# One layer of recurrent attention and routed experts on one core: how gathered rows are turned, how block 0 is projected, and how the recurrence is clipped

## The chip, the cores and the metric

The kernel runs on one core of a Trainium2 chip. The metric is the device time of one execution in microseconds (us). Before the change three runs gave a median of 363.4 us (362.94 to 363.56).

## What is computed

2048 tokens of 512 channels are normalized, and two branches are added to them:

```
xn = layernorm(x)                                  # (2048, 512), float32
r, v, k = split(xn @ W_rvk.T)                      # W_rvk (1536, 512)
for each token t:                                  # per channel; w = -exp(decay), u = first
    no = max(o, u + k);  A = exp(o - no);  B = exp(u + k - no)
    y  = (A * p + B * v) / (A * q + B)
    o2 = max(w + o, k);  A2 = exp(w + o - o2);  B2 = exp(k - o2)
    p, q, o = A2 * p + B2 * v,  A2 * q + B2,  o2
attention = (sigmoid(r) * y) @ W_out.T
probs = softmax(xn @ classifier.T)                 # 12 choices: 8 experts, 4 that hand xn through
top 2 of probs + bias, weights 1.5 * probs
ffn = sum of weight * down_e(silu(gate_e(xn)) * up_e(xn)) over a token's experts, + xn * weight of the 4
out = x + attention + ffn
```

## The kernel before

**Layout.** Tokens come in four blocks of 512 (TB). Each block is normalized row by row and turned on TensorE to xnT (channels on the partitions). The recurrence runs along the tokens, with 128 channels on the partitions, so there are 16 units (block b, channel group c); unit (b, c) needs (b-1, c). The rows of xn are also stored to DRAM (xs).

**Products k, v, r.** Direct products (half_k and project, L267 and L313) take four k-steps of 128x512 per output. For the rest, two outputs (k and v, or r of two channel groups) are made by seven products in place of eight (seven L476, sevens L560): sums of token halves (sum_tokens, S1 to S4) and of weights (T, R) are multiplied, each product is two k-steps of 256 columns, ScalarE copies the results from PSUM, and VectorE adds two of them later (the adds owed, L501, L624 and L637). In block 0, units 0 and 1 (LEAD = 2) are made directly, units 2 and 3 by seven, and r of all four directly.

**One unit's recurrence, scan(b, c), L336.** VectorE scans o2 = max(w + o, k) (L351), makes a2 = w + o - o2 (L353) and b2 = k - o2 (L354); ScalarE takes Exp of both (L356, L357); VectorE makes the two running sums (L363, L365), multiplies (L364), keeps the state (L372, L373), combines (L374 to L376), and later takes reciprocals (L380) and multiplies (L382). These steps are stages of a generator, given out one by one.

**Experts.** After routing, the places of the tokens are sorted by expert into 23 tiles of 128 rows; two are mixed from several experts. For tile i: gather (GpSimd's indirect DMA, token_i from L961) brings the rows xg; they are turned to xgT; up (L1096) multiplies them with the gate and up weights gw that SP has fetched (pg, 16 products of 128x128); activate takes Tanh and two VectorE operations; finish multiplies with dw (po) and scatters the rows, added to out. Tile 0 is turned on TensorE (turn, L1070: px, then a ScalarE copy). For all others flip (L1079) lets ScalarE split the float32 rows into their 16-bit halves (L1082), a DMA on SP's queue transposes the 16-bit array (L1084), and unite (L1087) lets ScalarE put the halves together (L1090).

**Order.** The whole is scheduled by hand: every engine runs its instructions in the order in which the program gives them out. Ahead of the experts, products are put between the routing steps with fill(n), owed adds with emit(n). Then a table (L1301 to L1338) of due times is filled by plan(): stages of the recurrence every UNIT, groups of four product steps, attention groups at places named in `after`, and the two halves of every tile every `spread`; it is sorted and given out. First_half(i) multiplies and activates tile i; second_half(i) unites tile i+1, flips i+2 and finishes i-1. k and v have five buffers each (kvp); the PSUM banks of p2, p3, pr and gu are single once block 0 is done. SP's queue holds, in order: the loads of x and the weights, the stores of xs, the weights gw and dw of tiles 0 and 1 (the second gw waits for which_late, L1272), then per tile flip, dw and gw. The last block's attention (L1244, L1232) ends the program.

Of the kernel before, what the change touches and what calls it, by code (L numbers as in the profile page):

```python
# [29 lines left out]
U16 = mybir.dt.uint16  # L30
# [5 lines left out]
P = 128  # L36
T = 2048
C = 512
# [21 lines left out]
QW = 32  # L60


@with_exitstack
def layer(ctx: ExitStack, tc: tile.TileContext, x, w_rvk, w_out, decay, first, cls, ebias, gu, down, out):
# [17 lines left out]
    dram = pool("dram", 1, space=bass.MemoryType.DRAM)  # L82
    psum = dict(space=bass.MemoryType.PSUM)
# [7 lines left out]
    def change_banks():  # L91
        early.close()
        for name, n in (("gu", 1), ("p2", 1), ("p1", 2), ("p3", 1), ("pr", 1)):
            banks[name] = pool(f"ps_{name}", n, **psum)
# [30 lines left out]
    load_w(2)  # L125
# [3 lines left out]
    load_x(2)  # L129
    load_w(1)  # L130
    load_x(3)
    load_w(0)
# [132 lines left out]
    first_k = {}  # L265

    def half_k(c, h):  # L267
        if h == 0:
            first_k[c] = ps_mm.tile([P, TB], F32, tag="mm", name=f"pk0_{c}")
        hs = slice(h * HALF, (h + 1) * HALF)  # L270
        for k in range(CC):
            nc.tensor.matmul(
                first_k[c][:, hs],
                wrvk_sb[2][:, k, c * P : (c + 1) * P],
                xnT[0][:, k, hs],
                start=(k == 0),
                stop=(k == CC - 1),
                skip_group_check=True,
            )
        if h == 1:  # L280
            kvr[0, c, "k"] = kvp.tile([P, TB], F32, tag="k", name=f"k0_{c}")
            nc.scalar.copy(kvr[0, c, "k"], first_k[c])
# [30 lines left out]
    def project(b, c, parts=(("k", 2), ("v", 1), ("r", 0))):  # L313

        n = f"{b}_{c}"
        for name, m in parts:
            ps = ps_mm.tile([P, TB], F32, tag="mm", name=f"p{name}{n}")
            for k in range(CC):
                nc.tensor.matmul(  # L319
                    ps,  # L320
                    wrvk_sb[m][:, k, c * P : (c + 1) * P],
                    xnT[b][:, k, :],
                    start=(k == 0),
                    stop=(k == CC - 1),
                )
                if k < CC - 1:
                    yield
            t = (erp if name == "r" else kvp).tile([P, TB], F32, tag=name, name=f"{name}{n}")
            if name == "r":
                nc.scalar.activation(t, ps, AF.Exp, scale=-1.0)  # L330
            else:
                nc.scalar.copy(t, ps)
            kvr[b, c, name] = t
            yield

    def scan(b, c):  # L336
# [9 lines left out]
        obv = wk1.tile([P, 3, TB + 1], F32, tag="obv", name=f"obv{n}")  # L346
        nc.vector.tensor_copy(obv[:, :, 0:1], s[:, 0:3].unsqueeze(2))
        o, bs, bvs = (obv[:, m, 0:TB] for m in range(3))
        o2, b2, bv = (obv[:, m, 1 : TB + 1] for m in range(3))
# [3 lines left out]
        nc.vector.scalar_tensor_tensor(a2, o, w, o2, ALU.add, ALU.subtract)  # L353
        nc.vector.tensor_sub(b2, k, o2)  # L354
        yield
        nc.scalar.activation(a2, a2, AF.Exp)  # L356
        nc.scalar.activation(b2, b2, AF.Exp)  # L357
# [3 lines left out]
        sums = wk1.tile([P, 2, TB], F32, tag="sums", name=f"sums{n}")  # L361
        sq, sp = sums[:, 0, :], sums[:, 1, :]
        nc.vector.tensor_tensor_scan(sq, bs, a2, s[:, 3:4], ALU.add, ALU.mult)  # L363
        nc.vector.tensor_mul(bv, b2, v)  # L364
# [3 lines left out]
        if b > 0:  # L368
            nc.scalar.activation(er, er, AF.Exp, scale=-1.0)
        num = yT[b][:, c, :]  # L370
        if b + 1 < NTB:
            nc.vector.tensor_copy(s[:, 0:3].unsqueeze(2), obv[:, :, TB : TB + 1])  # L372
            nc.vector.tensor_copy(s[:, 3:5].unsqueeze(2), sums[:, :, TB - 1 : TB])  # L373
        nc.vector.scalar_tensor_tensor(sq, b2, cf, sq, ALU.mult, ALU.add)  # L374
        nc.vector.scalar_tensor_tensor(er, er, 1.0, sq, ALU.add, ALU.mult)
        nc.vector.scalar_tensor_tensor(num, bv, cf, sp, ALU.mult, ALU.add)  # L376
        yield
        def divide(h):
# [45 lines left out]
    def sum_r_weights(first):  # L424
        if first:
            for n in (2, 3, 4):
                rsum[n] = sump.tile([P, 2, 2, P], F32, tag=f"R{n}", name=f"R{n}")
# [3 lines left out]
        else:  # L431
            nc.vector.tensor_add(rsum[2], rsum[3], r_weights(0, 0))
# [43 lines left out]
    def seven(b, c):  # L476

        n = f"{b}_{c}"
        cs = slice(c * P, (c + 1) * P)

        def bank(pool_, tag, name):
            return pool_.tile([P, TB], F32, tag=tag, name=f"{name}{n}")

        def place(pool_, name):
            kvr[b, c, name] = pool_.tile([P, TB], F32, tag=name, name=f"{name}{n}")
            return kvr[b, c, name]

        def multiply(ps, m, begin, end):
            a, w = factors(b, m)
            for k in range(2):  # L490
                nc.tensor.matmul(  # L491
                    ps[:, :HALF],
                    w[:, k, cs],
                    a[:, k, :],
                    start=(begin and k == 0),
                    stop=(end and k == 1),
                    skip_group_check=True,
                )

        def add(dst, src):  # L500
            nc.vector.tensor_add(dst, dst, src)  # L501

        def r_step(k):
            nc.tensor.matmul(  # L504
                pr, wrvk_sb[0][:, k, cs], xnT[b][:, k, :], start=(k == 0), stop=(k == CC - 1)
            )

        def next_sums(ns):
            if c == CC - 1 and b + 1 < NTB:
                for m in ns:  # L510
                    owe(lambda m=m: sum_tokens(b + 1, m))

        p1 = bank(ps_mm, "mm", "p1_")
        multiply(p1, 1, True, False)
        k = place(kvp, "k")
        nc.scalar.copy(k[:, :HALF], p1[:, :HALF])
        yield
        emit_owed()
        pr = bank(ps_tr, "tr", "pr")
        r_step(0)  # L520
        yield
        r_step(1)
        yield
        multiply(p1, 6, False, False)
        v = place(kvp, "v")
        nc.scalar.copy(v[:, :HALF], p1[:, :HALF])
        yield
        p3 = bank(ps_mm, "mm", "p3_")
        multiply(p3, 5, True, False)
        more = five.tile([P, TB], F32, tag="more", name=f"more{n}")  # L530
        nc.scalar.copy(more[:, HALF:], p3[:, :HALF])
        yield
        p2 = bank(ps_gu, "gu", "p2_")
        multiply(p2, 2, True, True)
        owe(lambda: add(k[:, :HALF], p2[:, :HALF]))
        next_sums((1, 2))
        yield
        multiply(p1, 7, False, False)
        nc.scalar.copy(v[:, HALF:], p1[:, :HALF])
        next_sums((3,))  # L540
        yield
        r_step(2)
        emit_owed()
        yield
        r_step(3)
        r = place(erp, "r")
        nc.scalar.activation(r, pr, AF.Exp, scale=-1.0)
        yield
        multiply(p1, 4, False, True)
# [3 lines left out]
        nc.scalar.copy(more[:, :HALF], p3[:, :HALF])  # L553
        owe(lambda: add(v, more))
        next_sums((4,))
        yield

# [851 lines left out]
```

## Time and profile before

| | |
|---|---|
| median of three runs | 363.4 us |
| the profiled execution | 362.48 us, its span 360.7 us, TensorE clock 1.00 |
| TensorE, VectorE, ScalarE, GpSimd busy | 354.0, 306.8, 159.0, 90.3 us |
| products pg of the tiles (L1109) | 79.1 us, products by seven (L592, nine groups) 129.8 us, attention (L1244) 54.1 us |
| ScalarE's copies for the turned rows | L1082 23.0 us (x22), L1090 25.6 us (x22) |
| VectorE's L354 / L351 / L363 / L365 | 11.0 / 20.4 / 20.5 / 20.6 us (x16 each) |
| DMA | 84.46 MB, 234 GB/s; packets of SP's queue 56.2% of 16 engines' span, of GpSimd's 25.1% |

The profile counts a float32 matmul as two instructions. A group's line reads: line, engine, operation, out<-in, shapes, count | busy us, mean ns of one | idle time before them and what ended it. The chain of work that ended last is followed back from the last instruction, in pieces of start, length and what. In a timeline a line is start, length, engine, line, operation. DVE is VectorE, ACT ScalarE, POOL GpSimd, PE TensorE, PEld its weight loads, SP the engine that issues most DMAs.

### The profile page before, as it was taken

Reading aid. Unit: us, or ns where it says so; the run is one execution under the profiler, and the core shown is the slowest. Engines: PE = TensorE matmul, PEld = TensorE weight load, DVE = VectorE, ACT = ScalarE, POOL = GpSimd, SP = SyncE. Lnnn points to the kernel's source line nnn. Section 1 sums busy time; section 2 is a strip of 40 time slices with the busy share of each in tenths; the row PEclk is TensorE's granted clock in tenths of the full one; section 3 lists DMA queues with packets and bytes.
Section 4 is the critical chain, followed back from the end, with each engine's and each line's share of the span. In section 5 each row is a group of like instructions: output and inputs, shape, how many; then the busy total and the mean of one; then the engine's idle time right before and its main releaser. Section 6 shows DMA issues by size and latency. Waiting matters only on the chain.

```text
span 360.7 us, 5328 instructions
## 1 busy us (share of the span) xinstructions
PE 354.0 (98%) x1850; PEld 256.7 (71%) x1850; DVE 306.8 (85%) x531; ACT 159.0 (44%) x308; POOL 90.3 (25%) x118
## 2 busy tenths in 40 slices
PE   8999999999999999999999999999999999999996
PEld 3764578799865877547877688988776988854344
DVE  5879889959999997899695799997989589979971
ACT  3576222354643645525545454546453546432000
POOL 6000300431312232321321433323322124221130
PEclk9999999999999999999999999999999999999999
DMA  8999950795869699967999968979979986924782
GB/s 282 398 356 363 331 174 2 245 323 135 254 196 248 147 367 301 276 215 189 281 281 334 294 189 216 309 147 306 284 226 262 236 173 167 337 55 58 177 139 95
DMA packets 47132, 84.46 MB, mean 234 GB/s; under 512 B 26496, under 2 KB 26880, under 8 KB 43328
## 3 DMA queue, kind: packets, MB, share of 16 engines
q1 hardware_dynamic: 39792, 64.05, 56.2%
q0 software_dynamic: 7312, 20.06, 25.1%
q8 instruction: 15, 0.25, 0.3%
q14 instruction: 13, 0.11, 0.1%
HBM read 63.25 MB, written 19.27 MB: 229 GB/s over the span
## 4 chain that ended last, share of the span: by engine, by line
PE 73%; DVE 17%; DMA 5%; ACT 2%; issue 1%; SPq 0%; DVEq 0%; ACTq 0%
PE pg L1109 19%; PE p L592 17%; PE po L1057 8%; PE pr L592 7%; PE pw L1244 7%; DVE r L380 4%; PE p L491 3%; DMA x<-in_x_dram 3%; DMA wrvk<-in_w_rvk_dram 2%; PE pr L504 2%; PE pr L319 2%; DVE sums L365 2%; DVE sums L363 2%; PE p2r L592 1%; PE po L1061 1%
## 5 line engine op out<-in xcount | busy, mean ns | idle before, releaser
L1109 PEld LDWEIGHTS pg<-xgT,gw 128*128 128x128 f32 x672 | 78.1, 192 | 3.7 <-ACT xgT L1090 1.6
L1109 PE MATMUL pg<-xgT,gw 128*128 128x128 f32 x672 | 79.1, 275 | 0.2 <-ACT xgT L1090 0.2
L1145 POOL DMA_INDIRECT out_dram<-yo,to_i x23 | 40.4, 1758 | 142.9 <-ACT yo L1141 28.7
L1244 PE MATMUL pw<-wout_sb,yT 128*128 128x512 f32 x120 | 54.1, 593 | 0.7 <-DVE xrows L1256 0.6
L380 DVE RECIPROCAL r<-r 128x256 f32<-128x256 f32 x32 | 53.7, 1719 | 0.0
L1244 PEld LDWEIGHTS pw<-wout_sb,yT 128*128 128x128 f32 x120 | 22.3, 190 | 25.5 <-issue 24.8
L1057 PE MATMUL po<-dw,act 128*128 128x512 f32 x84 | 39.5, 592 | 0.0
L1015 POOL DMA_INDIRECT xg<-xs,token_i x23 | 26.4, 1148 | 44.6 <-DVE empty L963 25.2
L1121 ACT ACTIVATE act<-pg 128x256 f32<-128x256 f32 x23 | 8.8, 384 | 65.0 <-PE pg L1109 60.4
L1122 DVE SCALAR_TENSOR_TENSOR act<-act,pg 128x256 f32<-128x256 f32 x23 | 9.6, 417 | 21.0 <-ACT act L1121 21.0
L1090 ACT COPY xgT<-xq 128x1024 uint16<-128x1024 uint16 x22 | 25.6, 1161 | 2.6 <-DMA xq<-xp 2.6
L1057 PEld LDWEIGHTS po<-dw,act 128*128 128x128 f32 x84 | 16.0, 190 | 13.7 <-issue 12.7
L592 PE MATMUL p<-xnT,wrvk 128*128 128x256 f32 x96 | 24.7, 380 | 0.7 <-DVE k L624 0.7
L592 PE MATMUL p<-S,wrvk 128*128 128x256 f32 x96 | 24.7, 380 | 0.0
L592 PE MATMUL p<-S,T 128*128 128x256 f32 x96 | 24.6, 379 | 0.0
L363 DVE TENSOR_TENSOR_SCAN sums<-obv,state,a 128x512 f32<-128x512 f32 x16 | 20.5, 1280 | 4.1 <-ACT obv L357 4.0
L1082 ACT COPY xp<-xg 128x1024 uint16<-128x1024 uint16 x22 | 23.0, 1047 | 0.0
L592 PEld LDWEIGHTS p<-xnT,wrvk 128*128 128x128 f32 x96 | 18.0, 190 | 6.0 <-issue 2.6
L592 PEld LDWEIGHTS p<-S,T 128*128 128x128 f32 x96 | 18.2, 190 | 5.0 <-issue 2.9
L365 DVE TENSOR_TENSOR_SCAN sums<-obv,state,a 128x512 f32<-128x512 f32 x16 | 20.6, 1288 | 0.6
L592 PEld LDWEIGHTS p<-S,wrvk 128*128 128x128 f32 x96 | 17.9, 190 | 4.3 <-issue 1.4
L351 DVE TENSOR_TENSOR_SCAN obv<-wdec,state,k 128x512 f32<-128x512 f32 x16 | 20.4, 1277 | 0.0
(262 smaller groups left out, 576.1 us busy)
## 6 DMA issues: line engine op xcount, KB each, us to landing
gw<-in_gu_dram SPq DMA_DIRECT2D x25, 1024.0 KB, 7.4
dw<-in_down_dram SPq DMA_DIRECT2D x25, 512.0 KB, 4.9
x<-in_x_dram SPq DMA_DIRECT2D x16, 256.0 KB, 6.4
xs<-x SPq DMA_DIRECT2D x16, 256.0 KB, 4.6
wrvk<-in_w_rvk_dram SPq DMA_DIRECT2D x3, 1024.0 KB, 7.2
xrow<-xs SPq DMA_DIRECT2D x8, 256.0 KB, 7.3
out_dram<-xrow POOLq DMA_DIRECT2D x8, 256.0 KB, 8.2
xrows<-xs SPq DMA_DIRECT2D x8, 256.0 KB, 6.4
```

The lines of the kernel that those rows point to most:

```text
L351: nc.vector.tensor_tensor_scan(o2, w.to_broadcast([P, TB]), k, s[:, 0:1], ALU.add, ALU.max)
L363: nc.vector.tensor_tensor_scan(sq, bs, a2, s[:, 3:4], ALU.add, ALU.mult)
L365: nc.vector.tensor_tensor_scan(sp, bvs, a2, s[:, 4:5], ALU.add, ALU.mult)
L380: nc.vector.reciprocal(er[:, hs], er[:, hs])
L592: nc.tensor.matmul(dst, rows_(k), a[:, k, :], start=(first and k == 0), stop=(k == 1), skip_group_check=True,)
L1015: nc.gpsimd.indirect_dma_start(out=xg, out_offset=None, in_=xs, in_offset=bass.IndirectOffsetOnAxis(ap=token[:, column(i) : column(i) + 1] ...
L1057: nc.tensor.matmul(out_, lhs[:, c, :], rhs[0][:, c, :], start=(c == 0), stop=(c == last))
L1082: nc.scalar.copy(xp, st[i]["xg"].bitcast(U16).rearrange("p (c h) -> p h c", h=2))
L1090: nc.scalar.copy(xgT.bitcast(U16).rearrange("p c (t h) -> p c t h", h=2), st[i]["xq"].rearrange("p (h c) t -> p c t h", h=2),)
L1109: nc.tensor.matmul(pg[:, c // IC, c % IC * P : (c % IC + 1) * P], w[0][:, k, rs], xgT[:, k, :], start=(k == 0), stop=(k == CC - 1),)
L1145: nc.gpsimd.indirect_dma_start(out=out, out_offset=bass.IndirectOffsetOnAxis(ap=index, axis=0), in_=yo[ps], in_offset=None, compute_op=ALU ...
L1244: nc.tensor.matmul(po, yT[b][:, c, j * P : (j + 1) * P], wout_sb[:, c, :], start=(c == 0), stop=(c == CC - 1),)
```

## The change

Three things change, with the due times around them.

1. **Rows turned by way of DRAM and VectorE.** turn on TensorE, flip and unite go. For every tile, spread_rows writes xg to DRAM as four column quarters (512-byte pieces), load_rows reads them back so that each group of 32 partitions holds one quarter of all 128 rows (2 KB per partition), and turn transposes 32x32 blocks on VectorE. The channels of the gate and up weights are permuted on the host to match. xgT has two buffers for one. turn(i+1) stands at the end of first_half(i), the load of tile i+2 and the write of i+3 in second_half(i).
2. **Block 0.** r of units 0 and 1 is multiplied first, in halves (half_r), then r of units 2 and 3 (project_r), and k and v of all four by seven products, interleaved (first_four). Weights are loaded in the order r, k, v, and block 3 of x ahead of k and v. More adds are owed ahead of the tiles: emit(2) before the weights of the choices, emit(4) for emit(2) after which_i.
3. **Clipping.** VectorE makes a2 = w + o - k, one operation; ScalarE makes b2 = Exp(-Relu(a2)) and then a2 = Exp(-Relu(-a2)), in two stages. L354 goes; the state is five columns of one tile and copied at once; the multiply with v stands before the first running sum. r of block 0 is copied, and Exp taken in scan.

The due times: UNIT 16.5 for 16.75, tiles from 8 on for 4, stages at (0, 4.5, 6, 7.5, 12, 14). The core of the diff:

```diff
@@ scan
-        obv = wk1.tile([P, 3, TB + 1], F32, tag="obv", name=f"obv{n}")
-        nc.vector.tensor_copy(obv[:, :, 0:1], s[:, 0:3].unsqueeze(2))
+        obv = wk1.tile([P, 5, TB + 1], F32, tag="obv", name=f"obv{n}")
+        nc.vector.tensor_copy(obv[:, :, 0:1], s.unsqueeze(2))
...
-        nc.vector.scalar_tensor_tensor(a2, o, w, o2, ALU.add, ALU.subtract)
-        nc.vector.tensor_sub(b2, k, o2)
+        nc.vector.scalar_tensor_tensor(a2, o, w, k, ALU.add, ALU.subtract)
         yield
-        nc.scalar.activation(a2, a2, AF.Exp)
-        nc.scalar.activation(b2, b2, AF.Exp)
+        nc.scalar.activation(b2, a2, AF.Relu)
+        nc.scalar.activation(b2, b2, AF.Exp, scale=-1.0)
         yield
+        nc.scalar.activation(a2, a2, AF.Relu, scale=-1.0)
+        nc.scalar.activation(a2, a2, AF.Exp, scale=-1.0)
+        yield
...
+        nc.vector.tensor_mul(bv, b2, v)
         nc.vector.tensor_tensor_scan(sq, bs, a2, s[:, 3:4], ALU.add, ALU.mult)
-        nc.vector.tensor_mul(bv, b2, v)
         nc.vector.tensor_tensor_scan(sp, bvs, a2, s[:, 4:5], ALU.add, ALU.mult)
...
-        nc.vector.scalar_tensor_tensor(sq, b2, cf, sq, ALU.mult, ALU.add)
-        nc.vector.scalar_tensor_tensor(er, er, 1.0, sq, ALU.add, ALU.mult)
+        nc.vector.scalar_tensor_tensor(a2, b2, cf, sq, ALU.mult, ALU.add)
+        nc.vector.scalar_tensor_tensor(er, er, 1.0, a2, ALU.add, ALU.mult)
@@ block 0
+    def first_four():
+        steps = {name: sevens(0, c, False)[0] for c, name in enumerate("ABCD")}
+        order = "A1 B1 A2 A6 B6 B2 A7 B7 A4 B4 C2 C1 D1 A5 D2 B5 C6 D6 A3 C7 B3 D7 C5 D5 C4 D4 C3 D3"
+        for name in order.split():
+            steps[name[0]][int(name[1])]()
+            yield
...
     def all_products():
-        for name, m in (("v", 1), ("r", 0)):
-            for u in range(LEAD):
-                yield from project(*units[u], ((name, m),))
-        for u in range(LEAD, CC):
-            yield from seven(*units[u])
+        for c in (2, 3):
+            yield from project_r(0, c)
+        yield from first_four()
@@ pair
+        if (b, c) == (1, 0):
+            order = "A1 R1 A2 A5 A6 R2 A3 A7 R5 R6 A4 B1 R7 R3 B6 B5 R4 B7 B3 B2 B4".split()
@@ routing
     nc.vector.tensor_scalar(far, real, -FAR, FAR, ALU.mult, ALU.add)
+    emit(2)
...
     which_i = place_tiles()
-    emit(2)
+    emit(4)
@@ tiles
+    def spread_rows(i):
+        q = dram_q.tile([P // SQ, P, P], F32, tag="quarters", name=f"quarters{i}")
+        nc.sync.dma_start(q.rearrange("g p c -> p g c"), st[i]["xg"].rearrange("p (g c) -> p g c", c=P))
+        st[i]["quarters"] = q
+
+    def load_rows(i):
+        xq = ex_p.tile([P, C], F32, tag="xq", name=f"xq{i}")
+        nc.sync.dma_start(xq, st[i]["quarters"].rearrange("g (i h) c -> (g i) (h c)", h=P // SQ))
+        st[i]["xq"] = xq
+
     def turn(i):
...
+        xgT = ex_p.tile([P, CC, P], F32, tag="xgT", name=f"xgT{i}")
+        nc.vector.transpose(
+            xgT.rearrange("p c (i h) -> p h c i", h=P // SQ),
+            st[i]["xq"].rearrange("p (h c j) -> p h c j", c=CC, j=SQ),
         )
         st[i]["xgT"] = xgT
@@ before the table
-    fill(4)
-    emit(3)
+    fill(2)
+    late = [owed.pop(0)[1] for _ in range(2)]
+    fill(3)
+    sum_tokens(1, 1)
+    sum_tokens(1, 2)
+    emit(1)
+    sum_tokens(1, 3)
+    sum_tokens(1, 4)
     sum_r_weights(True)
-    emit(1)
-    emit(1, 1)
     sum_r_weights(False)
-    emit(1)
-    mixed_tiles()
     head = False
-    fill(8)
-    turn(0)
-    flip(1)
+    fill(7)
+    for i in range(2):
+        spread_rows(i)
+    load_rows(0)
+    spread_rows(2)
+    load_rows(1)
@@ the table
-    for at in (-1, 3, 5, 10, 11.5):
+    for at in (-1, 2.5, 3.5, 5, 10, 11.5):
         plan(at, stages[0])
...
+    plan(2, mixed_tiles)
     plan(3, gather, 3)
+    plan(6.5, turn, 0)
+    for work in late:
+        plan(9, work)
...
-        plan(4 + spread * i, first_half, i, TILES)
-        plan(4 + spread * (i + 0.6), second_half, i, TILES)
+        plan(8 + spread * i, first_half, i, TILES)
+        plan(8 + spread * (i + 0.6), second_half, i, TILES)
```

## The prediction

> **What bounds the kernel now.** I read the page's busy shares first, then the chain of work that ended last, then the busy time by stretches, then the timelines around the first expert tile. All times are us from the start of the span.
>
> ```profile
> PE 354.0 (98%) x1850; PEld 256.7 (71%) x1850; DVE 306.8 (85%) x531; ACT 159.0 (44%) x308; POOL 90.3 (25%) x118
> ```
>
> TensorE is busy 98%, and this is no artefact of modelled ends: in the stretches below its starts follow each other at the pace of full work.
>
> ```profile
> 36.20:77.20 41.00, 41.00 (x197) 29.95 (x197) 37.87 (x111) 14.16 (x35) 9.43 (x12) 1.00 0.61 209
> 80.00:140.00 60.00, 59.29 (x343) 46.23 (x342) 58.16 (x85) 31.05 (x60) 14.37 (x10) 1.00 0.80 242
> 140.00:318.00 178.00, 177.78 (x985) 138.58 (x984) 151.27 (x214) 87.53 (x163) 51.21 (x37) 1.00 0.92 247
> ```
>
> The columns are span, then busy time of TensorE, weight loads, VectorE, ScalarE, GpSimd. TensorE lacks 0.9 us in 279 us. So a matmul removed is time gained, and a wait put in front of a matmul is time lost. VectorE has no room from 36 to 140 (its only wait from 36.2 to 77.2 is 0.4 us for ScalarE), and 27 us of room from 140 to 318. ScalarE and the DMA queues have room.
>
> The chain names the place that the change moves:
>
> ```profile
> 73.55 0.44 PE px L1074 x4
> 73.99 0.87 PE pr L592 x4
> 74.85 1.73 PE p L592 x8
> 76.58 3.58 PE pg L1109 x32
> 80.19 0.39 ACT act L1121
> ```
>
> Tile 0 is turned on TensorE itself (px), copied by ScalarE, and its first product pg starts without a wait. Two k-steps of a 128x256 product (x4 in the profile, which counts a float32 matmul twice) take 0.864 us (1.73 for x8).
>
> **Products saved: -2.2.** Of block 0, units 0 and 1 had k as 16 matmuls of 256 columns and v as 8 of 512, together 32 of 256; by sevens they are 28. Four at 0.432 us: -1.73. The four transposes of tile 0: -0.44. The r products are the same number, only earlier.
>
> **ScalarE: room.** It loses 22 copies L1082 (1.05 us) and 22 L1090 (1.16), and gains 32 Relu passes, bounded by the Exp rows L356/L357 (0.63) and, from below, by a 128x512 copy (0.57), so 18 to 20 us, and a few copies: about -24 in all. It was 44% busy, so I cost this at nothing. The changed program has two table loads, as before, so Relu brings none. The price of four passes is latency: the second Exp of a unit comes some 2.6 us after VectorE's a, not 1.3.
>
> **VectorE: +5.** Per unit it loses L354 (0.68) and a state copy (0.16), 16 times: -13. It gains four adds for units 0 and 1 (+2) and 23 transposes that the trace does not show. One pass over 128x512 float32 lies between the normalization L245 (0.54) and the scan (1.28); I take 0.68, the row of the plain two-operand pass L637, so 16 us, with 12 and 29 as ends. From 140 to 318 the 27 us of room hide that; from 80 to 140 the next paragraph makes room.
>
> **DMA and SP: even.** 22 transposes (issue to landing 4.6) give way to 23 writes to DRAM and 23 loads of 256 KB. The writes are bounded by xs<-x (4.6) and xrow<-xs (7.3), the loads likewise. In the steady state the write is issued a tile (some 10 us) before its load, and the load over half a tile before its transpose, so both are hidden; with that cover gone a tile would cost up to 5 us.
>
> **The first tile: +6.2, the step that decides.** Before, VectorE ran like this:
>
> ```profile
> 64.91 0.18 DVE L961 TENSOR_SCALAR token_i<-token 128x40 int32<-128x40 f32 x1
> 65.76 0.41 DVE L501 TENSOR_TENSOR k<-k,p 128x256 f32<-128x256 f32 x1
> 73.95 1.28 DVE L351 TENSOR_TENSOR_SCAN obv<-wdec,state,k 128x512 f32<-128x512 f32 x1
> 75.93 0.69 DVE L354 TENSOR_TENSOR obv<-k,obv 128x512 f32<-128x512 f32 x1
> 76.54 0.69 DVE L637 TENSOR_TENSOR v<-v,more 128x512 f32<-128x512 f32 x1
> ```
>
> In the changed program's order VectorE does this before tile 0 is turned:
> - two k adds ahead of the counting (0.74), and four k and v adds for two ahead of token_i (+0.93). The counting is dense, so the end of the token stage moves from 65.8 to 67.4. TensorE meets the first 0.74 at the products pi, where it had 0.3 to 0.4 spare on each of two, and the second at the first sum of block 1's tokens: +0.75 of wait in all.
> - then eight sums (5.2), three adds (1.3), the unit's first scan and a (2.05), mixed_tiles, which moves behind them (1.66): 77.6.
> - then, ahead of the transpose, the rest of unit (0,0): multiply 0.7, two scans 2.4, state copy 0.1, three combined operations 2.1, and some 0.8 of wait for ScalarE's second pair: 83.8. The transpose adds 0.65.
>
> The DMA path ends at the same time. Gather 0 was issued at 65.38 and took 4.2 us; with token_i 1.7 later it lands at 71.3. The write of its rows goes on SP's queue behind the weights of tiles 0 and 1: the second 1 MB waits for which_late on GpSimd, behind the gathers, and its two followers of 512 KB landed 7.6 us after issue at 69.3 and 69.9, so by 79.5 now. The write lands some 1 us later, 80.5; SP holds the load until then; a 256 KB load alone in the queue took 2.8, and behind the second tile's write a little more: 84.0.
>
> So xgT is there at 84.6, and pg starts at 84.7. TensorE has come to that point at 76.42 - 13.39 + 14.69 + 0.75 = 78.5: before, 1.72 of r, 13 steps of 0.864 and px stood between pi and pg; now 17 steps do, and the five buffers of k and v allow few more. The wait is 6.2 us. Queued behind pg on TensorE is everything; VectorE, too, then waits 4 us for the activation, and comes out some 5 us further ahead of TensorE than before.
>
> A rule of the Trainium skill speaks against this path: in "DMA: Bandwidth & Descriptors", rules for kernel authors, a DMA that reads what another wrote has to be issued after the first one's completion semaphore, for the queue does not order the two. With the rule the rows are loaded at 84.0; queued back to back they would be there near 81.5. VectorE is busy to 83.8 either way, so the sum goes by VectorE and stays.
>
> **What comes back: -1.6.** Before, TensorE waited 0.84 at 101.9 for a k add of the crowded VectorE, and 0.2 and 0.4 near 130 and 163 for xgT from ScalarE. With VectorE ahead and no ScalarE copies I take 1.2 of these back. In the tail, TensorE waited 0.3 and 0.7 before the last block's attention (pw at 343.15) for VectorE. From the last pg on, VectorE's chain for the last two units costs: the first loses nothing (multiply fills the wait for the second pair), the last pays 0.5 (two more passes, less L354 and the multiply moved up); but TensorE has 0.86 of product more there. Its wait shrinks from 1.0 to 0.6: -0.4.
>
> **The sum.** -2.2 + 0.75 + 6.2 - 1.2 - 0.4 = +3.2. The profiled execution took 362.48 (span 360.7), so 365.7 in its terms; the median of the runs is 363.4, so I forecast **366.6**. Its own range, from a transpose of 0.54 to 1.28 (0.6 on the first tile, 0 to 1 later) and from none to all of the 1.6 coming back: 365 to 368.5.
>
> **Rivals.**
> - *The first tile's rows are there in time* (chance 0.20). For it: TensorE has products to do, and SP and the DMA engines have gaps from 45 to 63. Against it: the sum of dense VectorE rows, and the weights ahead in SP's queue. Then only the savings remain: 363.4 - 2.2 + 0.75 - 1.6 = 360.4, faster. It decides at a wait of 3.0 us: with xgT before 81.5 the change gains.
> - *VectorE becomes the bound* (0.09): transposes of 1.28 add 13 us to my sum; the room from 140 to 318 takes most of it, but TensorE would wait at its one-buffer banks (p2 needs a VectorE add) for some 2 to 3: 369.5.
> - *The round trip is late beyond the start* (0.09): a write of 512-byte pieces lands 3 us later than I say, or SP, held by the load's wait, fetches the next weights late. One such wait of 3: 369.6.
> - Forecast: 0.62.
>
> **How the numbers follow.** The range 362.0 to 371.0 reaches up over both slower rivals with the upper bounds of their costs, and down to a first-tile wait of about 1.6; what it leaves out is most of the first rival (0.16) and the far end of the others (0.03). A measurement of this kernel can tell some 0.2% (0.7 us) from no change. Faster by more: 0.18, from the first rival. Within: 0.07, from its edge and the forecast's lower edge. Slower: 0.75.
>
> **What would show it.** In the changed profile: TensorE's idle before tile 0's pg, 5 to 7 us, put down to VectorE's xgT, at 78 to 85; the transposes' mean near 0.7; VectorE waiting some 4 us for the first activation; no wait near 102; TensorE at pw of the last block some 3 us later. I am wrong if pg starts before 81, or if TensorE waits again at every tile.

## The result and the profile after

Four executions of the changed kernel took 377.6, 378.1, 378.6 and 383.2 us, median 378.35; the kernel before, run on the same chip, took 363.25 (362.94 to 363.56). The ratio is 1.0444, 95% interval 1.0356 to 1.0532: slower by some 15 us, where +3.2 was forecast. The profiled execution took 378.13 us, its span 376.1 (before: 362.48 and 360.7), so 15.4 us of span are to be found. The longest of the four also has the lowest mean TensorE clock (0.977, the others 0.982 to 0.986).

The page of the changed kernel; first the busy times, then the granted TensorE clock in 40 slices of 9.4 us:

```profile
PE 356.9 (95%) x1870; PEld 265.2 (71%) x1870; DVE 318.6 (85%) x530; ACT 139.2 (37%) x307; POOL 89.4 (24%) x118
...
PEclk9999999996997999999999999999999999999999
```

TensorE is busy 95%, not 98%, and its clock dips in slices 10 and 13. From 120 to 340 it is busy 20.00 us of every 20, so the loss lies before that. Two places hold most of the loss, as TensorE's timeline shows (start, duration, then in brackets the idle time before and what ended it):

```profile
80.37 1.03 PE L514 MATMUL p<-S,T 128*128 128x256 f32 x4
86.44 5.77 PE L1038 MATMUL pg<-xgT,gw 128*128 128x128 f32 x32 [5.05 <-issue]
92.05 1.03 PE L514 MATMUL p<-S,wrvk 128*128 128x256 f32 x4
...
104.26 1.88 PE L989 MATMUL po<-dw,act 128*128 128x512 f32 x4
111.76 2.07 PE L514 MATMUL p<-xnT,wrvk 128*128 128x256 f32 x4 [5.62 <-DVE k L549]
113.63 1.91 PE L514 MATMUL pr<-S,wrvk 128*128 128x256 f32 x4
115.34 4.95 PE L1038 MATMUL pg<-xgT,gw 128*128 128x128 f32 x32
```

The first wait is the forecast one, for tile 0's turned rows xgT, which VectorE ends at 86.34 (below). The second stood before with 0.68 us and is now 5.62: product 2 of unit (1,2) writes the single bank p2, which is free only when VectorE has added the product of unit (1,1) to its k ("the k add" from here on). And behind each wait the same work takes longer: pg of a tile, 3.73 us before, takes 5.77 and 4.95, a product 2.07 for 1.03. The stretches right behind the two waits (span, then busy time of TensorE, weight loads, VectorE, ScalarE, GpSimd, then granted clock, DMA share, GB/s):

```profile
84.00:90.00 6.00, 3.56 (x17) 3.58 (x18) 2.34 (x3) 0.00 (x0) 2.36 (x2) 0.50 0.99 341
112.00:118.00 6.00, 6.00 (x22) 5.25 (x22) 5.67 (x5) 0.37 (x1) 2.30 (x2) 0.51 0.84 195
```

The clock records say 0.5 from 83.74 to 90.57 and from 111.04 to 117.87, 6.83 us each; before had no such stretch while it ran. VectorE's timeline shows why both waits end so late:

```profile
79.12 0.69 DVE L360 TENSOR_TENSOR obv<-obv,v 128x512 f32<-128x512 f32 x1 [0.94 <-ACT obv L353]
...
84.61 0.75 DVE L371 SCALAR_TENSOR_TENSOR yT<-obv,cfac 128x512 f32<-128x512 f32 x1
85.27 1.07 DVE L1019 STREAM_TRANSPOSE xgT<-xq 128x512 f32<-128x512 f32 x1
92.67 0.42 DVE L1051 SCALAR_TENSOR_TENSOR act<-act,pg 128x256 f32<-128x256 f32 x1 [6.33 <-ACT act L1050]
...
104.93 0.75 DVE L371 SCALAR_TENSOR_TENSOR yT<-obv,cfac 128x512 f32<-128x512 f32 x1
105.59 3.36 DVE L376 RECIPROCAL r<-r 128x256 f32<-128x256 f32 x2
...
110.38 1.08 DVE L1019 STREAM_TRANSPOSE xgT<-xq 128x512 f32<-128x512 f32 x1
111.30 0.41 DVE L549 TENSOR_TENSOR k<-k,p 128x256 f32<-128x256 f32 x1
```

VectorE stands 6.33 us with everything queued behind tile 0's activation, then is dense from 92.67 to 111.7 but for two waits for ScalarE (0.76 and 0.49 us), and the 0.41 us that TensorE needs is the last thing in that row, behind unit (0,1), a division, an activation and a transpose.

Where the 15.4 us are (some waits are given "start to start": by how much a matmul starts later than the usual distance behind the one before it, which is a little more than the idle time in brackets): the start +0.75 (the first product begins at 9.88, before at 9.13; in the profiles of experiments 2 and 3 it begins at 8.99 and 9.23, so this part changes from execution to execution); two waits for ScalarE copies and one for a sum ahead of tile 0 +2.1 (0.62, 1.21, 0.26, start to start); tile 0's rows +5.05; half clock behind them +2.0 (5.77 less 3.73); the k add +4.9 (5.62, less 0.68 before); half clock behind it +3.05 (two products and pg take 3.58 and 4.78 where 1.73 and 3.58 would do); products saved -2.1 (an estimate: all matmuls of the profile, each at the median distance of its kind, add up to 341.15 us before and 339.07 after); small waits of before that are gone -0.6. The sum is 15.15; the rest is in differences too small to name.

### The profile page after: what moved, and what is told of

The parts are those of the page before. It is cut to its first block, busy times and chain, and to the rows that moved or that the text cites. A ratio compares the mean times of both kernels' runs of the same rounds, so it can differ in the third digit from the quotient of the medians.

```text
span 376.1 us, 5348 instructions
## 1 busy us (share of the span) xinstructions
PE 356.9 (95%) x1870; PEld 265.2 (71%) x1870; DVE 318.6 (85%) x530; ACT 139.2 (37%) x307; POOL 89.4 (24%) x118
## 4 chain that ended last, share of the span: by engine, by line
PE 62%; DVE 18%; issue 2%; ACT 2%; DVEq 0%
PE pg L1038 19%; PE p L514 15%; PE pw L1175 8%; PE po L989 8%; PE pr L514 7%; DVE r L376 3%; PE pg L993 2%; DVE obv L347 1%; PE p2r L514 1%; DVE obv L361 1%; PE po L993 1%; DVE tok L857 1%; DVE v L562 1%; DVE obv L362 1%; DVE xgT L1019 1%
## 5 line engine op out<-in xcount | busy, mean ns | idle before, releaser
L1038 PEld LDWEIGHTS pg<-xgT,gw 128*128 128x128 f32 x672 | 81.7, 199 | 8.3 <-issue 6.9
L514 PE MATMUL p<-xnT,wrvk 128*128 128x256 f32 x128 | 33.5, 389 | 5.6 <-DVE k L549 5.6
L514 PEld LDWEIGHTS p<-xnT,wrvk 128*128 128x128 f32 x128 | 24.5, 195 | 13.0 <-DVE k L549 6.5
L514 PE MATMUL p<-S,wrvk 128*128 128x256 f32 x128 | 32.9, 382 | 0.1
L514 PE MATMUL p<-S,T 128*128 128x256 f32 x128 | 32.4, 379 | 0.0
L514 PEld LDWEIGHTS p<-S,wrvk 128*128 128x128 f32 x128 | 23.6, 190 | 6.7 <-issue 2.7
L514 PEld LDWEIGHTS p<-S,T 128*128 128x128 f32 x128 | 23.9, 190 | 4.7 <-issue 1.9
L361 DVE TENSOR_TENSOR_SCAN obv<-obv,state,a 128x512 f32<-128x512 f32 x16 | 20.5, 1283 | 7.5 <-ACT a L356 7.5
L1070 ACT ACTIVATE yo<-po,wplace 128x512 f32<-128x512 f32 x23 | 15.8, 687 | 29.3 <-PE po L989 26.2
L1019 DVE STREAM_TRANSPOSE xgT<-xq 128x512 f32<-128x512 f32 x23 | 25.6, 1115 | 0.0
L362 DVE TENSOR_TENSOR_SCAN obv<-obv,state,a 128x512 f32<-128x512 f32 x16 | 20.2, 1263 | 0.0
```

The lines of the kernel that those rows point to most:

```text
L362: nc.vector.tensor_tensor_scan(sp, bvs, a2, s[:, 4:5], ALU.add, ALU.mult)
L514: nc.tensor.matmul(dst, rows_(k), a[:, k, :], start=(first and k == 0), stop=(k == 1), skip_group_check=True,)
L1019: nc.vector.transpose(xgT.rearrange("p c (i h) -> p h c i", h=P // SQ), st[i]["xq"].rearrange("p (h c j) -> p h c j", c=CC, j=SQ),)
L1038: nc.tensor.matmul(pg[:, c // IC, c % IC * P : (c % IC + 1) * P], w[0][:, k, rs], xgT[:, k, :], start=(k == 0), stop=(k == CC - 1),)
L1070: nc.scalar.activation(yo, po, AF.Identity, scale=weight[:, column(i) : column(i) + 1])
```

## The experiments

Theory T, later O: the loss is two TensorE waits and the half clock behind them, and the second comes from the order of VectorE's queue. Against it stood V (VectorE has too much work there, in whatever order), D (the DMA round trip is slow in itself) and P (the parts that stay, sevens and Relu, cost the time). Times are medians; each ratio, with its 95% interval, is to runs of the kernel before on the same chip. Executions of one kernel differ by several us wherever TensorE waits long, and each profile shows one of them.

**1. Rows early.** SP's queue and one due time:

```diff
     fetch(0)
+    spread_rows(0)
+    load_rows(0)
     fetch(1, 0, which_late[0:1, 0:1])
...
-    plan(6.5, turn, 0)
+    plan(3, turn, 0)
```

> Edit: tile 0's round trip (write to DRAM, load) goes on SP's queue right behind tile 0's weights instead of behind the weights of both first tiles, and VectorE turns it before the second stage of unit (0,0), not after it. Theory T (two TensorE waits, each followed by about 6.8 us of half clock: 5.05 + 2.07 us at tile 0's pg, 5.62 + 3.05 us at the k add near 106 to 112, the rest small waits before tile 0): rows there near 78, pg(0) near 81.5, no wait and no half clock there; VectorE and TensorE both come 6.5 to 7 us earlier, so the second wait stays as long as it was: 378.1 - 7.1 = 371.0 us. Rival V (VectorE has too much to do up to 112, so time won at tile 0 comes back at the k add): second wait 11 to 13 us, 377 to 378. Rival D (the DMA round trip itself is slow, wherever it is queued): pg(0) not before 84, 376 or more.

373.32 us, ratio 1.0296 (1.0267 to 1.0325). pg(0) starts at 81.40 without a wait or half clock: the round trip is fast where no weights are queued ahead, D falls. TensorE came 5.3 us sooner to the k add and waited longer there:

```profile
107.49 2.08 PE L514 MATMUL p<-xnT,wrvk 128*128 128x256 f32 x4 [6.68 <-DVE k L549]
```

VectorE had in turn stood 2.74 us for tile 1's rows. So the wait grew by 1.1, and the gain was 5.0, not 7.1.

**2. Division later.**

```diff
-        divide_some(2)
+        if i > 1:
+            divide_some(2)
         activate(i)
...
         fetch_parts("d", i)
+        if i == 1:
+            divide_some(2)
```

> Edit: of the first finished unit, the division (two reciprocals and a product, 4.05 us of VectorE) is put behind the k add that TensorE waits for near 106 to 112, instead of ahead of tile 1's activation. Theory T: the wait shrinks from 5.6 to about 1.6 us, the half clock behind it (3.05 us) goes, the first wait stays: 378.1 - 4.0 - 3.05 = 371.0 us. Rival V: VectorE has as much to do as before, so TensorE meets the 4 us at the next k or v add or at the next transpose: 375 to 378. If the half clock comes without a long wait, 374.

381.75 us, 1.0469 (1.0384 to 1.0555): no gain. The k add's wait shrank to 1.59 as forecast, and TensorE stopped 4.5 us later for 3.32, behind a ScalarE copy (last line):

```profile
108.17 1.13 PE L514 MATMUL p<-xnT,wrvk 128*128 128x256 f32 x4 [1.59 <-DVE k L549]
112.62 1.65 PE L514 MATMUL pr<-S,wrvk 128*128 128x256 f32 x3 [3.32 <-ACT r L533]
...
112.20 0.37 ACT L533 COPY r<-pr 128x256 f32<-128x256 f32 x1 [8.65 <-DVE yT L378]
```

This copy of r stood 8.65 us itself, for yT L378, the end of the division: r has six buffers, and the division that was moved back frees the one this copy fills. The division is owed as early as the k add. This left V standing.

**3. TensorE kept busy in the first wait.**

```diff
         xgT, w = st[i]["xgT"], st[i]["w"]
+        if i == 0 and 0 in cs:
+            for _ in range(20):
+                nc.tensor.matmul(pg, ones, ones.unsqueeze(1).to_broadcast([P, TB // P, P]), start=True, stop=True)
```

> Edit: 20 matmuls that nothing uses (bf16, 128x512, about 4.4 us at full clock) stand ahead of tile 0's pg, into its bank, so that TensorE is not idle in the first wait. The output is unchanged. Theory T: pg(0) starts at the same 86.4, the granted clock stays 1.0 through 83 to 91, pg(0) takes 3.7 instead of 5.8 us, the second wait is a little longer as VectorE's end is what it waits for but starts from an earlier activation too: 378.1 - 2.0 = 376.1 us, or 376 to 377. If the half clock has another cause than TensorE's idleness (load of other engines, DMA traffic): it is there again and the time stays at 378 or is above it.

377.13 us, 1.0418 (1.0365 to 1.0471). pg(0) starts at 85.91, and the clock stays:

```profile
86.00:92.00 6.00, 6.00 (x44) 5.72 (x45) 1.79 (x4) 1.13 (x3) 0.52 (x1) 1.00 0.94 334
```

So the half clock comes from TensorE's idleness, under the same DMA and VectorE load. The gain from end to end, 1.2 us of medians where 2.0 was forecast, is inside the interval; the k add's wait (5.61) remained.

**4. Tiles turned as before** (L1001 to L1024 and their calls replaced by those of the kernel before: px and a copy for tile 0, DMA transposes and two ScalarE copies for the others).

> Edit: one part of the change undone: tile 0 is turned on TensorE, the other tiles by the DMA transpose with ScalarE's two copies, as in the kernel before; the products by sevens, the later r and the Relu clipping stay. Theory T (the round trip and the order it forces on VectorE make both long waits; the rest of the change costs the 3 us of small waits ahead of tile 0 and saves 2): no half clock, no wait over 2 us after 76, 364 us, 362 to 367. Rival P (the parts that stay make the second wait: four ScalarE passes, the later adds): the wait near 106 is still 4 us or more, 369 to 373.

369.57 us, 1.0187 (1.0157 to 1.0217). No wait at tile 0, no transposes on VectorE, and still:

```profile
104.09 2.08 PE L515 MATMUL p<-xnT,wrvk 128*128 128x256 f32 x4 [4.25 <-DVE k L550]
```

The second wait thus comes neither from the first nor from the transposes. It is in what stayed: the order, the sevens or Relu.

**5. The k add and the transpose first.**

```diff
-    def owe(work):
-        owed.append((clock[0] + 2, work))
+    def owe(work, steps=2):
+        owed.append((clock[0] + steps, work))
...
-            owe(lambda: nc.vector.tensor_add(t["k"][:, :HALF], t["k"][:, :HALF], src))
+            owe(lambda: nc.vector.tensor_add(t["k"][:, :HALF], t["k"][:, :HALF], src), 1)
...
+        if i + 1 < n:
+            turn(i + 1)
         divide_some(2)
         activate(i)
-        if i + 1 < n:
-            turn(i + 1)
```

> Edit, VectorE's order alone: a k add is due one product after the product it adds, not two, which puts the one that TensorE waits for near 106 ahead of unit (0,1)'s second stage; and a tile's transpose stands ahead of the division and the activation of the tile before it, not behind. The round trip and the first wait stay. Theory O (order: TensorE stands still because the one short instruction that it needs, a k add or a transpose, is queued on VectorE behind some 10 us of unit work that nobody needs yet): k add near 98.5, transpose of tile 2 near 106, no wait and no half clock from 92 to 120: 378.1 - 5.6 - 3.05 = 369.4 us. Rival V (VectorE simply has more work up to 112 than TensorE, whatever the order): TensorE waits 4 us or more at another VectorE result between 98 and 125, 374 or more.

375.91 us, 1.0368 (1.0317 to 1.0419), 6.5 us over the forecast. The k add came at 98.82 and nobody waited for it; the wait moved to the r copy once more, 3.13 us without a half clock:

```profile
111.03 1.13 PE L514 MATMUL pr<-S,wrvk 128*128 128x256 f32 x4 [3.13 <-ACT r L533]
```

**6. Experiments 1 and 5 together.**

> Edit: the early rows of the first experiment and the VectorE order of the experiment beside this one, together. Theory O: neither long wait; tile 1's rows land near 89 and hold VectorE, so tile 2's transpose ends near 104 and TensorE waits 1.6 us for it, no half clock: 373.3 - 5.1 - 3.05 - 1.1 = 364 us, 363 to 366. Rival V: the waits add up to 6 us again, 370 or more.

374.7 us, 1.0341 (1.0321 to 1.0361): a miss by 10 us. Tile 1's rows held VectorE 4.37 us, with act(0) now behind the transpose, and TensorE waited 5.12 us at 107.66, again for the r copy. Three things stand in one row on VectorE (k add, division, transpose), and all three are due; putting two first leaves the third.

**7. Experiment 4 with k adds early and the tiles earlier.**

```diff
-        plan(8 + spread * i, first_half, i, TILES)
-        plan(8 + spread * (i + 0.6), second_half, i, TILES)
+        plan(5 + spread * i, first_half, i, TILES)
+        plan(5 + spread * (i + 0.6), second_half, i, TILES)
```

(and k adds due one product sooner, as in 5). On VectorE this puts the division (90.58 to 94.66) and the k add (95.97) ahead of unit (0,1)'s second stage (96.30).

> Edit: the fourth experiment (tiles turned as in the kernel before; sevens, order of the first products and Relu as in the changed one), with k adds due one product sooner and the tiles' halves planned 3 units of TensorE time earlier (5, not 8). Theory O: the k add ends near 97.5, TensorE comes to its successor near 100.6 without a wait, no half clock: 369.6 - 4.2 - 3.0 = 362.4 us, 361.5 to 364, about even with the kernel before (363.2), as the saved products are paid for by the small waits ahead of tile 0. Rival P (the sevens and the Relu passes cost the time): 367 or more.

363.35 us, 1.0022 (1.0002 to 1.0041): 6.2 us under experiment 4 by order alone. From 80 to 120 TensorE is idle 0.06 us, at full clock:

```profile
80.00:100.00 20.00, 19.94 (x119) 17.69 (x120) 18.92 (x27) 13.55 (x27) 2.05 (x2) 1.00 0.60 186
100.00:120.00 20.00, 20.00 (x116) 14.06 (x116) 17.44 (x27) 11.18 (x21) 4.85 (x4) 1.00 0.83 235
```

P falls as the cause of the second wait.

**8. Relu undone in the changed kernel.**

```diff
-        nc.vector.scalar_tensor_tensor(a2, o, w, k, ALU.add, ALU.subtract)
+        nc.vector.scalar_tensor_tensor(a2, o, w, o2, ALU.add, ALU.subtract)
+        nc.vector.tensor_sub(b2, k, o2)
...
-        nc.scalar.activation(b2, a2, AF.Relu)
-        nc.scalar.activation(b2, b2, AF.Exp, scale=-1.0)
+        nc.scalar.activation(b2, b2, AF.Exp)
         yield
-        nc.scalar.activation(a2, a2, AF.Relu, scale=-1.0)
-        nc.scalar.activation(a2, a2, AF.Exp, scale=-1.0)
+        nc.scalar.activation(a2, a2, AF.Exp)
```

> Edit: the Relu part of the change undone inside the changed kernel: VectorE clips again by two operations on o (one 128x512 operation of 0.69 us more per unit), ScalarE makes one Exp pass for each of the two, not Relu and Exp. Theory O: VectorE's waits for the second pair (0.94 and 0.76 in unit (0,0), 0.76 and 0.49 in unit (0,1)) give way to 0.69 of work each, so pg(0) near 85.5 and the k add near 110: 378.1 - 1 to 2 us, 376 to 378. Rival P: the Relu passes are a main cost: 374 or less.

381.06 us, 1.0534 (1.049 to 1.0578), but executions lay between 374.5 and 383.6, with mean clocks from 0.986 down to 0.973: not to be read in this kernel. Both long waits were there (4.52 and 5.02 us).

**9. Rows early, k add and division before the second stage**: experiment 1, with k adds due one product sooner and the tiles at 5, and turn(i+1) ahead of the division for i > 0.

> Edit: the round trip and the products as in the changed kernel, early rows and early k adds as in the sixth experiment, and the tiles' halves planned 3 units of TensorE time earlier (5, not 8), so that on VectorE the division of unit (0,0), the activation of tile 1 and the k add stand ahead of unit (0,1)'s second stage; ScalarE's copy of the next r, which takes over the division's buffer, is then free near 99.5. Theory O (order of VectorE's queue): what is left after 81 us are waits of 1.6, 1.4 and 1.4 us (tile 1's rows, a k copy, the k add), none long enough for a half clock: 372.8 - 12.0 + 4.4 = 365.2 us, 364 to 367. Rival V (VectorE's work before 112, whatever the order): 6 us and more of waits again, 370 or more.

368.22 us, 1.0139 (1.0121 to 1.0157): 5 us less than 1, 3 more than forecast. VectorE now stood for rows twice:

```profile
88.19 1.09 DVE L1019 STREAM_TRANSPOSE xgT<-xq 128x512 f32<-128x512 f32 x1 [2.50 <-DMA xq<-quarters]
...
95.25 1.15 DVE L1019 STREAM_TRANSPOSE xgT<-xq 128x512 f32<-128x512 f32 x1 [2.21 <-DMA xq<-quarters]
```

and the k add came 2.80 us late for TensorE, with a half clock behind that wait. Tile 0's round trip had taken 5.5 us in all (write issued at 70.44, load landed at 75.92); tile 1's, behind the weights, 12 (76.19 to 88.16).

**10. Experiment 9 with the products of block 1's first pair apart.**

```diff
-            order = "A1 R1 A2 A5 A6 R2 A3 A7 R5 R6 A4 B1 R7 R3 B6 B5 R4 B7 B3 B2 B4".split()
+            order = "A1 R1 A2 A5 A6 R2 A3 A7 R5 A4 R6 B1 R7 B6 B5 R3 B7 R4 B3 B2 B4".split()
```

> Edit: the kernel of the experiment beside this one, and in block 1's first pair the products R5 and R6, and R7 and R3, which write one bank that ScalarE must first read, stand two products apart, not one behind the other. Theory O: the waits of 0.62 and 1.21 us for ScalarE ahead of tile 0 go, as another product stands beside each copy; tile 0's rows are there in time: 1.2 to 1.8 us less than the kernel beside, 363.5 us. If the early waits only move to tile 0's rows, no change.

370.46 us, 1.0217 (1.0196 to 1.0237): 7 us over the forecast and 2.2 over experiment 9. The ScalarE waits of 0.62 and 1.21 went, and TensorE met tile 1's rows earlier instead, 2.48 us with a half clock behind it (pg 5.44):

```profile
90.63 5.44 PE L1038 MATMUL pg<-xgT,gw 128*128 128x128 f32 x32 [2.48 <-issue]
```

The profiled spans of 10 and 9 are alike (366.8 and 366.6); the products apart are a gain only if the rows are there.

**11. Experiment 7 with the same products apart.**

> Edit: the seventh experiment (tiles turned as in the kernel before, sevens and Relu as changed, k adds early, halves at 5) with the products of block 1's first pair apart, as in the experiment beside. Theory O: 363.35 less 1.2 to 1.8 us, 361.8 us: about 1 us under the kernel before, whose products it has 2.2 us less of, less 1 us of waits. Rival: the wait for the first tile's copies takes its place: 363.3.

361.7 us, 0.9965 (0.995 to 0.998): as forecast, under the kernel before. Behind the first matmul TensorE is nowhere idle for 0.9 us or more.

**12. Relu alone, in the kernel before.**

```diff
-        nc.vector.scalar_tensor_tensor(a2, o, w, o2, ALU.add, ALU.subtract)
-        nc.vector.tensor_sub(b2, k, o2)
+        nc.vector.scalar_tensor_tensor(a2, o, w, k, ALU.add, ALU.subtract)
         yield
-        nc.scalar.activation(a2, a2, AF.Exp)
-        nc.scalar.activation(b2, b2, AF.Exp)
+        nc.scalar.activation(b2, a2, AF.Relu)
+        nc.scalar.activation(b2, b2, AF.Exp, scale=-1.0)
+        nc.scalar.activation(a2, a2, AF.Relu, scale=-1.0)
+        nc.scalar.activation(a2, a2, AF.Exp, scale=-1.0)
```

> Edit: one part of the change alone, put into the kernel before: a is o + w - k, ScalarE clips it by Relu on both sides in two pairs of passes, VectorE's second subtraction goes; everything else as before. Theory O: VectorE is spared 0.69 us per unit, but its second stage waits 1.3 us longer for ScalarE's four passes where it is behind, so the k add near 102 comes 0 to 1 us sooner or later; later it is off the path: 363 us, 362 to 364. Rival P (the Relu passes cost the time): 365 or more.

369.04 us, 1.0154 (1.0129 to 1.0178), against theory O. The k add is not the place (0.2 us of wait); tile copies on ScalarE are (pg waited 1.07 and 1.55 us, start to start, at 120 and 165), and the tail:

```profile
349.23 3.65 PE L1245 MATMUL pw<-wout_sb,yT 128*128 128x512 f32 x4 [3.00 <-DVE xrows L1257]
```

where the last unit's VectorE stage waits for all four passes (0.56 before), and a half clock follows. All four stood in one step here; the change splits them in two steps, and has no tile copies. So this run prices the passes in one block, not the change's Relu.

**13. Experiment 9 with the rows of tiles 1 and 2 early too.**

```diff
     fetch(0)
     spread_rows(0)
+    spread_rows(1)
     load_rows(0)
     fetch(1, 0, which_late[0:1, 0:1])
+    load_rows(1)
     for i in range(2):
         fetch_down(i)
...
     plan(3, turn, 0)
+    plan(3.5, load_rows, 2)
```

(and the later calls for these rows go).

> Edit: the ninth experiment, with the rows of tiles 1 and 2 also queued early on SP: tile 1's write and load right behind tile 0's (its load behind tile 1's weights), tile 2's load ahead of the weights of the third part. Theory Q (what is left of the loss is the place of these transfers in SP's queue): xq of tile 1 lands near 82 and of tile 2 near 87, VectorE no longer stands 2.5 and 2.2 us for them, the k add ends near 97.5, TensorE waits for nothing from 80 to 120: 368.2 - 0.7 - 3.0 - 1.5 (half clock) = 363 us, 362.5 to 364.5, even with the kernel before. Rival S (the round trip's and the transposes' standing cost of 5 us): 367 or more.

363.74 us, 1.0039 (1.0017 to 1.0062). All three parts of the change are in it, all 23 transposes included:

```profile
80.00:100.00 20.00, 20.00 (x125) 17.80 (x125) 19.68 (x28) 8.58 (x20) 3.25 (x3) 1.00 0.81 282
100.00:120.00 20.00, 20.00 (x112) 13.93 (x112) 18.08 (x27) 8.39 (x19) 5.11 (x4) 1.00 0.92 285
```

TensorE is never idle from 80 to 120 while VectorE does 37.8 of 40 us: V falls, the work fits in, barely, if its order is right. How barely, the executions show: nine of the ten took 362.62 to 365.99 us, one took 374.77, at a mean clock of 0.991; what waited in that one is not recorded. Rival S, a standing cost of the round trip, falls too.

**14. The same with the products apart.**

> Edit: the kernel of e13 with the products R5 and R6, R7 and R3 of block 1's first pair two apart, as in the tenth experiment. Theory Q: TensorE comes to tile 0 some 1.5 us sooner, the rows of tile 1 are there: 361.5 to 363 us. Rival S: 366 or more.

363.29 us, 1.0025 (1.0007 to 1.0043), 0.3 above the forecast and no clear gain over 13: 1.03 us of wait (start to start) for tile 0's turned rows took the place of the ScalarE waits, as in 10.

**15. Experiment 11 with the old clipping** (the edit of 8).

> Edit: the eleventh experiment (361.7 us) with VectorE clipping as in the kernel before (one operation of 0.69 us more per unit on VectorE, ScalarE one Exp pass for two passes). Theory O (the Relu part is neutral once no wait hangs on it): 361 to 362.5 us. Rival P (Relu's four passes cost): 360.5 or less; if they gain by sparing VectorE: 363 or more.

360.62 us, 0.9948 (0.9931 to 0.9965), 0.4 under the forecast range and 0.1 above what rival P asked for. Its interval overlaps that of 11, so Relu in two pairs costs between nothing and some 1.5 us here. Its one longer wait, 2.48 us idle at 175.71 for weights (gw), was 0.82 in experiment 11.

## Why the prediction was wrong, step by step

- **Products saved, -2.2.** Right as far as it can be read: the estimate from the two profiles above is 2.1, and experiment 11, with these savings and hardly a wait, is 1.3 us under before. No run has this part alone.
- **ScalarE: room, at nothing.** Busy time fell by 19.8 (159.0 to 139.2), near the 24 forecast, and no table load was added. But the share hid two places: TensorE waited 0.62 and 1.21 us (start to start) for ScalarE copies ahead of tile 0, because products that write one bank stand back to back in the new order, and the second copy stood behind the unit's Relu and Exp. That is +1.8 that the sum lacks; the order of experiments 10 and 11 took it away, but for 0.37 us in 11.

  ```profile
  74.63 1.13 PE L514 MATMUL pr<-S,R 128*128 128x256 f32 x4 [0.46 <-ACT morer L545]
  79.40 1.13 PE L514 MATMUL pr<-S,wrvk 128*128 128x256 f32 x4 [1.05 <-ACT r L553]
  ```
- **VectorE, +5 and absorbed.** Busy time rose by 11.8. The transpose is the term that was mis-sized, 1.115 us for 0.68, inside its bounds:

```profile
L1019 DVE STREAM_TRANSPOSE xgT<-xq 128x512 f32<-128x512 f32 x23 | 25.6, 1115 | 0.0
```

  The amount did no harm: experiment 13 has all of it and no wait from 80 to 120.
- **DMA and SP even.** True of the steady state in the profile after. In the profiles of experiments 2 and 3, VectorE stood 2.4 and 1.7 us near 261 for rows queued behind a megabyte of weights, and TensorE 2.7 us behind it: the third rival's mechanism, in some executions.
- **The first tile, +6.2.** The mechanism was right, with VectorE, not DMA, at the end: rows landed at 84.12 (84.0 forecast), unit (0,0)'s stage ended at 85.3 and xgT at 86.3 (83.8 and 84.6). By the forecast's own numbers the rows, not VectorE, came last by 0.2 us (84.0 and 0.65 make its 84.6), though it says that the sum goes by VectorE. The wait was 5.05, as TensorE came at 81.4, not 78.5, for the waits named above. The Trainium skill's rule weighed there ("DMA: Bandwidth & Descriptors", rules for kernel authors: a DMA that reads what another wrote is issued after the first one's semaphore) agrees with the trace: the load was issued at 81.29, after the write had landed at 81.14. What the path would take without that wait, no run here shows.
- **The order ahead of tile 0, +0.75, and what comes back, -1.6.** Of the 0.75, TensorE lost 0.2 us at the products pi and 0.26 at the sum (start to start). Of the 1.2 that should come back 0.6 did, the waits of pg for ScalarE's copies; the 0.84 for the k add grew instead, by the step that failed. In the tail TensorE's two waits before pw were 0.31 and 0.72 and are 0.31 and 0.66, so 0.1 came back there, not 0.4.
- **The step that failed** is "VectorE, too, then waits 4 us for the activation, and comes out some 5 us further ahead of TensorE than before", and with it "no wait near 102" and the 1.2 that come back. VectorE did wait, 6.33 us, but a wait in front of a full queue puts everything behind it later, and does not move VectorE ahead. From the start of pg(0) VectorE needed 4.2 us to the activation and 21.2 to the end of the k add before, 6.2 and 19.0 after: 25.4 and 25.3. The profile before has, for TensorE and VectorE:

  ```profile
  76.42 3.73 PE L1109 MATMUL pg<-xgT,gw 128*128 128x128 f32 x32
  101.85 1.13 PE L592 MATMUL p<-xnT,wrvk 128*128 128x256 f32 x4 [0.68 <-DVE k L624]
  ...
  80.61 0.42 DVE L1122 SCALAR_TENSOR_TENSOR act<-act,pg 128x256 f32<-128x256 f32 x1 [3.38 <-ACT act L1121]
  101.38 0.41 DVE L624 TENSOR_TENSOR k<-k,p 128x256 f32<-128x256 f32 x1
  ```

  TensorE had 24.6 us to do in that stretch before (76.42 to 101.0), 19.7 after (86.44 to 106.14), 2 of these half clock. 25.3 - 19.7 is the wait, 5.6. What shrank is TensorE's side: four more products stand ahead of pg(0) and tile 2's pg behind the k add, 7 us. The prediction counted "17 steps" for 13 and used them for tile 0 alone.
- **The term that was missing** is the half clock, 5 us behind two waits. That a wait makes the work behind it dearer is in no line of the sum. The Trainium skill has it: "TensorE: Matmul & The Clock Gate", Part 1, names half rate as the state after one idle window or more of some 3.4 us, and says that the window is free-running. The traces agree on the window: every stretch at one clock, up to the last change, is a whole number of 3.41 us (in the profile after 23, 2, 6, 2 and 76 of them). They do not agree that a whole window must be idle. Laid on these windows, 15 at full clock in which TensorE was idle 2.02 us (experiment 9) to 3.41 us were each followed by a window at half clock, and none in which it was idle 1.93 us (experiment 6) or less was. So the 2.48 us of experiment 10, all in the window from 88.16 to 91.57, cost a half clock, and the 3.13 us of experiment 5, from 107.90 to 111.03, did not: the border at 109.58 parts them into 1.68 and 1.45. This is read from these profiles, whose matmul ends are modelled; no run was made to find the limit.
- **The rivals.** "VectorE becomes the bound" named the right place, a bank that needs a VectorE add, with 2 to 3 us for 5.6, and the wrong cause: without the transposes the wait was 4.25 (experiment 4), with them and another order none (experiment 13).

By experiments: order and queue places at the start are worth 14.6 us (378.35 to 363.74 with every part of the change in), and what remains is some 1 us over the kernel before. Left open: how much Relu in two pairs costs in the reordered kernels, between nothing and some 1.5 us, and what each of the three things that experiment 13 mends in the order is worth alone, since each alone only handed the wait on.

## What to carry to other kernels

When products are moved ahead on one in-order engine, do not stop at the wait they meet first: for every later hand-over, set side by side what each engine has queued between the two, since a short add behind ten microseconds of unhurried work is as late as that work. A TensorE wait of more than some 2 us is to be priced with the chance of half speed for the work behind it, 2 to 3 us each in the profile after; from 4.2 us on every wait here had it. A transfer's own time (5.5 us for a write and a read back) says little if 2 MB of weights stand ahead of it in the queue.

## What the hardware showed that was not expected

- While there was work, half-clock stretches lasted 3.41 or 6.83 us, nothing between: one or two windows. All TensorE gaps of 4.2 us or more that ended in real work had one behind them, those of 1.6 us or less none; gaps of 2.48 to 3.32 us had one where 2.02 us or more fell into one window, and none where the border parted them. A second half-clock window followed the first where TensorE was idle in that one for 0.69 us or more (eight times), and full clock where it was idle for 0.43 us or less. Twenty matmuls that nobody reads kept the clock at 1.00 (experiment 3).
- A VectorE transpose of 128x512 float32 in blocks of 32 took 1.115 us, against 0.69 for a two-operand pass and 1.27 for a scan over as many elements (profile after).
- The same 256 KB round trip took 5.5 us with nothing ahead of it in SP's queue (tile 0 of experiment 9) and 11 to 12 us behind weights (tile 0 in the profile after, tile 1 of experiment 9).
